# Mixture-of-experts FFN behind an adaptive layer norm: six of eight token blocks sorted by expert

## The chip, the cores and the metric

The kernel runs on one core of one Trainium2 chip. The metric is the device time of one execution in microseconds (us). Of the kernel before there are three timed runs: 565.57, 567.19 and 568.79 us, median 567.19. One more execution was profiled; it took 565.48 us, of which the traced span is 563.4 us.

Engines: PE multiplies matrices, DVE and POOL do elementwise work, ACT does activations and copies, SP only issues DMAs. POOL issues DMAs as well in the changed kernel. Each engine works through its own queue in order.

## The reference

There are 4096 tokens (128 batches of 32) of 128 features, all in fp32. Two layers, each a conditioning step and a feed-forward step with a residual:

```python
# layer 0: conditioning
U = (mu @ W_dec + b_dec).reshape(B, IN_DIM + 1, K)          # K = 30
param = jnp.einsum('bik,kj->bij', U, V)
out = jnp.einsum('bsd,bde->bse', x, param[:, :-1, :]) + param[:, -1, :][:, None, :]
# layer 0: mixture of 8 experts, the best two of each token
topk_scores, topk_idx = jax.lax.top_k(xf @ Wg.T + bg, K)    # K = 2
w = jax.nn.softmax(topk_scores, axis=-1)
h = jax.nn.gelu(jnp.einsum('td,ehd->teh', xf, W1) + b1[None], approximate=False)
o = jnp.einsum('teh,eoh->teo', h, W2) + b2[None]            # all experts, hidden 256
out = jnp.einsum('tko,tk->to', jnp.take_along_axis(o, topk_idx[:, :, None], axis=1), w)
# layer 1: conditioning by table look-ups, three layer norms and an MLP; then
h = jax.nn.silu(_tlin(x, w1_w, w1_s)) * _tlin(x, w2_w, w2_s)          # 128 -> 512
h = jax.nn.gelu(_tlin(h, h1_w, h1_s), approximate=False)              # 512 -> 512
h = jax.nn.gelu(_tlin(h, h2_w, h2_s), approximate=False)              # 512 -> 512
out = _tlin(h, w3_w, w3_s)                                            # 512 -> 128
```

A token needs only two experts of eight; computing all eight gives the same sum with six weights of zero.

## The kernel before

The tokens are split into NB = 8 blocks of TB = 512. Features lie on the partitions, tokens along the free dimension.

**Setup.** The conditioned token of layer 0 has rank 30, so `conditioned(i)` (L221) computes a 32-row vector z per token (`pz`, L225; `zT`, L233), splits it into a rounded half and a remainder [...], and stacks it four times over 128 partitions (`z4s[i]`, L245). `folded_all` (L210) folds V and W1 into `w4`. The gate scores `pg` (L308) come from `z4s`; `routing` (L252) is a chain of some 30 DVE operations over [128, 32 x 8] that finds the best two experts of every token and writes their weights into `hot4` (L300, L301).

**Experts.** `experts(i)` (L473) goes through all 8 experts for its 512 tokens. For each expert: one matmul `pbc` (L491) that spreads the token's weight for this expert over the partitions; and for both 128-row halves of the hidden layer a matmul `ph` (L495, fp32r), a Gelu on ACT (`hs`, L497), a product with `pbc` on DVE (`hw`, L499), and a matmul in full fp32 that accumulates into `po` (L500). The fp32 matmul appears as two records in the trace.

**Conditioning.** `conditioning(i)` (L511) makes the input of the second feed-forward step from `x1T`: transposes, three layer norms (`layernorm`, L394, with two small POOL operations L402 and L403; the norm of `h` also scales its four tiles on POOL, L405), table look-ups as one-hot matmuls (`ppw`, L542), an MLP (`pi`, L577 to L596) and the result `cT` (L608). `halves` (L617) splits it: a cast on ACT (L620) and a subtraction on POOL (L622).

**Feed-forward.** `feed_forward(i)` (L631) has four layers. `pf` gives four `ga` tiles through `gated` (L625: one ACT and two DVE operations each), then `pgb` and `pgc` give four tiles each with a Gelu on ACT (L666). All these matmuls are fp32r at L638, and each activation is split by `halves` for the layer after it. At the end `oT` (L677), a transpose `pot` (L680), a copy and a store.

**Order.** The generators yield between steps, and `beside` (L51) interleaves the streams given to it in proportion to their step counts. A scheduler that works with estimated durations then lays the instructions out on each engine, the earlier emitted first where several are ready; on the chip each queue is fixed. The main loop runs three streams at a time and waits for all of them:

```python
for i in range(NB):
    streams = [(feed_forward(i), 14)]
    if i + 1 < NB: streams.append((conditioning(i + 1), 13))
    if i + 2 < NB: streams.append((experts(i + 2), 18))
    beside(*streams)
```

Before it `experts(0)` runs beside the loading of the feed-forward weights (L360, a POOL sum at L369) and the small second-layer weights (L422), then `experts(1)` beside `conditioning(0)`.

Of the kernel before, what the change touches and what calls it, by code (L numbers as in the profile page):

```python
# [16 lines left out]
P = 128  # L17
# [13 lines left out]
VPW = 125  # L31
EPS = 1e-5
# [18 lines left out]
def beside(*streams):  # L51


    left = [[s, n, 0] for s, n in streams]
    while left:
        e = min(left, key=lambda e: (e[2] + 0.5) / e[1])
        e[2] += 1
        if next(e[0], e) is e:
            left.remove(e)
# [3 lines left out]
def adaln_ffn_kernel(ctx: ExitStack, tc: tile.TileContext, a, out: bass.AP):  # L63
# [32 lines left out]
    def rows(tag, n):  # L96

        t = const.tile([P, n], F32R, tag=tag, name=tag)
        nc.gpsimd.memset(t.bitcast(F32), 0.0)
        return t  # L100
# [12 lines left out]

    early = ctx.enter_context(ExitStack())
    setup = early.enter_context(tc.tile_pool(name="setup", bufs=1))
# [8 lines left out]
    bias_rows = load("bias_rows", [1, E * H + E], eng=nc.scalar, pool=setup)  # L124
    w1_t = load("moe_w1", [D, E * H], pool=setup)
    x_all = setup.tile([D, NB, TB], F32, tag="x_all", name="x_all")
    for i in range(NB):
        nc.sync.dma_start(x_all[:, i, :], a["x_t"][:, i * TB : (i + 1) * TB])
    tabs = load("tabs", [4 * E, NTAB], eng=nc.scalar, pool=setup)
    vecs = load("vecs", [P, NVEC], eng=nc.scalar)  # L130
    w2_t = load("moe_w2", [P, E, NH, D])
    int_w1 = load("int_w1", [P, 6, D], a["int_w1"].rearrange("(i p) j -> p i j", p=P))
    aw_bc = load("aw", [P, 6], a["aw"].partition_broadcast(P), eng=nc.scalar)
    st_a = load("st_a", [64, 4, D], eng=nc.scalar)
    st_b = load("st_b", [32, 2, D], eng=nc.scalar)
    wide_w2 = load("wide_w2", [D, 4, D])
    b2_rows = load("b2_rows", [1, 3 * D], eng=nc.scalar)
    tab_b = load("tab_b", [D, 3, 16], eng=nc.scalar)
# [17 lines left out]
    def stacked(dst, src, r, tmp):  # L156
# [3 lines left out]
        hi = tmp.tile([n, dst.shape[1]], F32R, tag="hi", name=f"hi_{dst.tensor.name}", bufs=2)  # L160
# [8 lines left out]
    twice = const.tile([2 * KZ, 2, 2 * KZ], F32R, tag="twice", name="twice")  # L169
# [31 lines left out]
    g4 = const.tile([P, E], F32R, tag="g4", name="g4")  # L201

    def folded(dst, w, bias, name):
        n = dst.shape[1]
        pv = ps_acc(name)
        nc.tensor.matmul(pv[:, :n], pre[:, V4 : V4 + P], w, start=True, stop=False)
        nc.tensor.matmul(pv[:, :n], bias_at, bias, start=False, stop=True)
        stacked(dst, pv[:, :n], 64, setup)

    def folded_all():  # L210
        folded(g4, pre[:, WG : WG + E], bias_rows[:, E * H :], "pgv")
# [38 lines left out]
    hot4 = const.tile([P, NCH, 4, E], F32, tag="hot4", name="hot4")  # L250

    def routing(pg):  # L252

        def t8(name, dt=F32):
# [590 lines left out]
```

## Time and profile before

| | us |
|---|---|
| median of three runs | 567.19 |
| the profiled execution | 565.48 |
| its span, first to last instruction | 563.4 |
| setup and routing, up to the first `pwT` | 0 to 63.4 |
| experts 0 and 1, conditioning 0, up to the first `cT` | 63.4 to 143.1 |
| feed-forward 0 to 5, each beside experts and conditioning | 143.1 to 476.9 |
| feed-forward 6 beside conditioning 7 | 476.9 to 518.9 |
| feed-forward 7 alone, and the end | 518.9 to 563.4 |

Busy share of the span: PE 88%, DVE 51%, ACT 42%, POOL 37%. In the profile, busy time of PE counts each matmul with its passage through the array, and neighbours overlap; how long PE needs per matmul is read from the distance between the ends of successive ones. "PEclk" is the granted clock of PE, 1.00 being full speed. A wait is put down to the instruction that released it.

### The profile page before, as it was taken

The page shows a single profiled execution, that of the slowest core. Times are in us where ns is not written, and L with a number is a line of the kernel's source. Part 1 is how long each engine was busy: PE and PEld are TensorE (multiplying, and loading weights), DVE is VectorE, ACT ScalarE, POOL GpSimd, SP SyncE. Part 2 cuts the span into 40 slices and gives each one's busy share as a digit, 9 for nine tenths or more (in the row PEclk, how much of TensorE's full clock was granted, in tenths as well). Part 3 has the DMA queues.
Part 4 walks back from the last instruction along what each step waited for, and adds up shares of the span by engine and source line. Part 5 has one row for each costly group of instructions (what it writes and reads, how often), then busy time and mean ns, then how long its engine had stood idle before and what let it go on. Part 6 is the DMA issues. An engine that isn't in the chain of part 4 may idle for free. (4 is left out here: it accounts for less than half of the span.)

```text
span 563.4 us, 5941 instructions
## 1 busy us (share of the span) xinstructions
PE 497.5 (88%) x1997; PEld 310.3 (55%) x1997; DVE 289.0 (51%) x689; ACT 235.4 (42%) x412; POOL 209.4 (37%) x226
## 2 busy tenths in 40 slices
PE   5998587979899979997999799979997999689694
PEld 5963243534566546654665466546654665365373
DVE  2875786744763565356535653565356535623400
ACT  0141553322455344534453455345534552353343
POOL 3000065030373237323722372237223722384353
PEclk9985599989899999999999999999999999899588
DMA  8800330100100020002000200020001000100100
GB/s 209 298 11 3 113 110 1 39 19 5 53 19 2 2 74 19 0 3 74 19 1 3 74 19 0 5 74 18 1 1 57 0 1 1 56 0 1 37 0 24
DMA packets 14634, 20.46 MB, mean 36 GB/s; under 512 B 1632, under 2 KB 7358, under 8 KB 14342
## 3 DMA queue, kind: packets, MB, share of 16 engines
q1 hardware_dynamic: 13762, 19.56, 10.9%
q10 hardware_dynamic: 836, 0.47, 0.4%
q8 instruction: 18, 0.29, 0.2%
q14 instruction: 18, 0.14, 0.1%
HBM read 13.72 MB, written 6.29 MB: 36 GB/s over the span
## 5 line engine op out<-in xcount | busy, mean ns | idle before, releaser
L500 PE MATMUL po<-hw,moe_w_sb 128*128 128x512 f32 x256 | 135.8, 627 | 8.7 <-DVE hw L499 8.7
L499 DVE TENSOR_TENSOR hw<-hs,pbc 128x512 f32<-128x512 f32 x128 | 85.9, 681 | 67.7 <-PE pbc L491 35.0
L497 ACT ACTIVATE hs<-ph 128x512 f32<-128x512 f32 x128 | 74.6, 596 | 55.2 <-PE ph L495 31.8
L622 POOL TENSOR_TENSOR gc_lo<-gc,gc_hi 128x512 fp32r<-128x512 f32 x32 | 40.7, 1273 | 95.8 <-ACT gc_hi L620 95.2
L500 PEld LDWEIGHTS po<-hw,moe_w_sb 128*128 128x128 f32 x256 | 44.2, 193 | 48.4 <-DVE hw L499 36.5
L622 POOL TENSOR_TENSOR ga_lo<-ga,ga_hi 128x512 fp32r<-128x512 f32 x32 | 41.0, 1280 | 68.9 <-ACT ga_hi L620 68.9
L495 PE MATMUL ph<-z,w 128*128 128x512 f32 x128 | 53.2, 442 | 2.5 <-ACT hs L497 2.5
L622 POOL TENSOR_TENSOR gb_lo<-gb,gb_hi 128x512 fp32r<-128x512 f32 x32 | 40.5, 1287 | 18.8 <-ACT gb_hi L620 16.6
L638 PE MATMUL pgc<-gb_lo,f_h_hi 128*128 128x512 f32 x128 | 44.8, 454 | 1.4 <-POOL gb_lo L622 1.3
L638 PE MATMUL pgb<-ga_hi,f_h_hi 128*128 128x512 f32 x128 | 42.7, 447 | 1.3 <-DVE sl L628 1.3
L666 ACT ACTIVATE gb<-pgb,vecs_sb 128x512 f32<-128x512 f32 x32 | 22.0, 689 | 50.1 <-PE pgb L638 50.1
L638 PE MATMUL pgc<-gb_hi,f_h_hi 128*128 128x512 f32 x128 | 41.0, 437 | 0.1
L666 ACT ACTIVATE gc<-pgc,vecs_sb 128x512 f32<-128x512 f32 x32 | 22.0, 689 | 45.4 <-PE pgc L638 45.4
L627 ACT ACTIVATE sl<-pf,half_w1s 128x512 f32<-128x512 f32 x32 | 22.0, 688 | 43.8 <-PE pf L638 41.1
L638 PE MATMUL pf<-cT_hi,f_w_hi 128*128 128x512 f32 x64 | 32.8, 534 | 8.3 <-DVE sl L628 5.9
L638 PE MATMUL pgb<-ga_lo,f_h_hi 128*128 128x512 f32 x128 | 39.4, 422 | 0.1
L491 PE MATMUL pbc<-w_rows,pick 128*128 128x512 f32 x64 | 36.9, 577 | 0.0
L628 DVE SCALAR_TENSOR_TENSOR sl<-sl,pf 128x512 f32<-128x512 f32 x32 | 21.7, 679 | 20.5 <-ACT sl L627 20.3
L638 PEld LDWEIGHTS pgb<-ga_hi,f_h_hi 128*128 128x128 f32 x128 | 24.8, 196 | 12.9 <-issue 4.1
L638 PEld LDWEIGHTS pgc<-gb_lo,f_h_hi 128*128 128x128 f32 x128 | 24.1, 188 | 13.9 <-issue 6.0
L495 PEld LDWEIGHTS ph<-z,w 128*128 128x128 f32 x128 | 24.9, 196 | 12.1 <-ACT hs L497 6.5
L638 PE MATMUL pf<-cT_lo,f_w_hi 128*128 128x512 f32 x64 | 27.8, 442 | 3.7 <-POOL cT_lo L622 3.6
(230 smaller groups left out, 810.2 us busy)
## 6 DMA issues: line engine op xcount, KB each, us to landing
moe_w_sb<-in_moe_w_dram SPq DMA_DIRECT2D x2, 1024.0 KB
x_all<-in_x_t_dram SPq DMA_DIRECT2D x8, 256.0 KB
xT<-in_x_t_dram SPq DMA_DIRECT2D x8, 256.0 KB
f_h_raw<-in_f_h_dram SPq DMA_DIRECT2D x8, 256.0 KB
kept_x<-x1T SPq DMA_DIRECT2D x8, 256.0 KB
kept_c<-cT SPq DMA_DIRECT2D x8, 256.0 KB
out_dram<-o SPq DMA_DIRECT2D x8, 256.0 KB
pid<-in_pid_dram SPq DMA_DIRECT2D x8, 250.0 KB
```

Source lines behind the costliest of these rows:

```text
L491: nc.tensor.matmul(pbc, pick[:, e, :], wr, start=True, stop=True)
L495: nc.tensor.matmul(ph, w4[:, c : c + P], z4, start=True, stop=True)
L497: nc.scalar.activation(hs, ph, AF.Gelu)
L499: nc.vector.tensor_tensor(hw, hs, pbc, ALU.mult)
L500: nc.tensor.matmul(po, w2_t[:, e, h, :], hw, start=False, stop=(e == E - 1 and h == NH - 1))
L622: nc.gpsimd.tensor_tensor(lo, src, hi, ALU.subtract)
L627: nc.scalar.activation(tmp, p1, AF.Tanh, scale=half_w1s[:, f : f + 1])
L628: nc.vector.scalar_tensor_tensor(tmp, tmp, 1.0, p1, ALU.add, ALU.mult)
L638: nc.tensor.matmul(dst, w[:, c, f * P : (f + 1) * P], src[c][h], start=(k == 0), stop=(k == len(terms) - 1),)
L666: nc.scalar.activation(t, ph, AF.Gelu, scale=col(s + f))
```

## The change

- Blocks 0 and 1 keep the dense path over all experts. For blocks 2 to 7 the z vectors are transposed to one row per token (`z_tok`), and `sorting` computes on the chip, for each of a token's two experts, its place in that expert's list (a matmul with a triangle of ones, and a prefix sum over the 24 groups of 128 tokens).
- 48 indirect DMAs, issued by POOL, scatter the rows of z (256 B each, 128 rows per DMA) into `z_rows` in DRAM, which was zeroed by eight DMAs from SP. Each expert has a fixed CAP of 1024 rows.
- `sorted_expert` runs 16 tiles of 512 rows, two per expert: two loads of the rows, four transposes, two `ph` matmuls, two Gelus, eight pairs' worth of 128-wide fp32 matmuls into `py`, an add of the bias, and a store to `y_rows` in DRAM.
- `combined(i)` reads the block's rows back: eight indirect DMAs per block on POOL, each followed by a DVE multiply-add onto x; then four transposes give `x1T`. In these blocks the first layer norm reads the sum directly, so the transposes at L522 are not made.
- The gate scores come from `zT` in full fp32 instead of the stacked z. The norm of `h` is scaled on DVE instead of POOL.
- The streams are put in order by start and length in a virtual time (`in_order`), no longer in groups that wait for each other. Conditioning i ends half a unit ahead of feed-forward i.
- If an expert gets more than 1024 rows, a conditional block at the end computes blocks 2 to 7 again by the dense path. With these inputs the six blocks give the experts 766, 662, 729, 818, 757, 715, 929 and 768 rows, so it isn't entered.

The core of the diff:

```diff
--- before.py
+++ after.py
+ND = 2
+NS = NB - ND
+TS = 512
+CAP = 1024
+ALL = NS * TB
+NT_S = E * CAP // TS
...
-def beside(*streams):
-    left = [[s, n, 0] for s, n in streams]
-    while left:
-        e = min(left, key=lambda e: (e[2] + 0.5) / e[1])
-        e[2] += 1
-        if next(e[0], e) is e:
-            left.remove(e)
+def in_order(*streams):
+    times = [(t + d * k / n, j) for j, (t, d, n, _) in enumerate(streams) for k in range(n)]
+    for _, j in sorted(times):
+        next(streams[j][3], None)
+    for *_, s in streams:
+        for _ in s:
+            raise ValueError("more steps than were given")
...
+    x_t = []
+    for i in range(NB):
+        x_t.append(setup.tile([D, TB], F32, tag=f"x_t{i}", name=f"x_t{i}"))
+        nc.sync.dma_start(x_t[i], a["x_t"][:, i * TB : (i + 1) * TB])
     w1_t = load("moe_w1", [D, E * H], pool=setup)
-    x_all = setup.tile([D, NB, TB], F32, tag="x_all", name="x_all")
-    for i in range(NB):
-        nc.sync.dma_start(x_all[:, i, :], a["x_t"][:, i * TB : (i + 1) * TB])
+    z_rows = kept.tile([E * ALL, 2 * KZ], F32, tag="z_rows", name="z_rows")
+    zeros = setup.tile([P, TB], F32, tag="zeros", name="zeros")
+    nc.gpsimd.memset(zeros, 0.0)
+    for e in range(E):
+        nc.sync.dma_start(
+            z_rows[e * ALL : e * ALL + CAP].rearrange("(p c) k -> p (c k)", p=P), zeros
+        )
...
+        pv = ps_acc("pgv")
+        nc.tensor.matmul(
+            pv[:KZ, :E], pre[:, V4 : V4 + KZ], pre[:, WG : WG + E], start=True, stop=False
+        )
+        nc.tensor.matmul(
+            pv[:KZ, :E], bias_at[:, :KZ], bias_rows[:, E * H :], start=False, stop=True
+        )
...
+        for c in range(NC):
+            nc.tensor.matmul(
+                pg[:, (i * NC + c) * E : (i * NC + c + 1) * E],
+                zT[:, c * P : (c + 1) * P],
+                gv,
+                start=True,
+                stop=True,
+            )
...
+            pt = ps_mm(f"pzt_{i}")
+            for c in range(NC):
+                nc.tensor.transpose(
+                    pt[:, c * KZ : (c + 1) * KZ], zT[:, c * P : (c + 1) * P], ident[:KZ, :KZ]
+                )
+            z = z_tok[i - ND]
+            both = pt[:, : NC * KZ].rearrange("p (c k) -> p c k", k=KZ)
+            nc.scalar.copy(z[:, :, 0, :], both)
+            nc.vector.tensor_tensor(z[:, :, 1, :], both, z[:, :, 0, :], ALU.subtract)
+            nc.sync.dma_start(
+                z_kept[i - ND].rearrange("(c p) k -> p c k", p=P),
+                z.rearrange("p c r k -> p c (r k)").bitcast(F32),
+            )
...
+    def sorting(hots):
+        n, c0 = NS * NC, ND * NC
+        h = [t[:, c0:] for t in hots]
+        both = setup.tile([P, n, E], F32R, tag="both", name="both")
+        nc.vector.tensor_tensor(both, h[0], h[1], ALU.add)
+        flat = both.rearrange("p c e -> p (c e)")
+        pr = ps_mm("p_rank")
+        nc.tensor.matmul(pr[:, : n * E], before, flat, start=True, stop=True)
+        pn = ps_ff("p_count")
+        nc.tensor.matmul(pn[:, : n * E], ones_r, flat, start=True, stop=True)
+        src, dst = sums
+        nc.vector.tensor_copy(src[:, PRE:], pn[:, : n * E].rearrange("p (c e) -> p c e", e=E))
+        d = 1
+        while d < n:
+            nc.vector.tensor_tensor(
+                dst[:, PRE:], src[:, PRE:], src[:, PRE - d : PRE - d + n], ALU.add
+            )
+            src, dst = dst, src
+            d *= 2
+        row = setup.tile([P, n, E], F32, tag="row", name="row")
+        nc.vector.tensor_tensor(
+            row,
+            pr[:, : n * E].rearrange("p (c e) -> p c e", e=E),
+            src[:, PRE - 1 : PRE - 1 + n],
+            ALU.add,
+        )
+        row_z = setup.tile([P, n, E], F32, tag="row_z", name="row_z")
+        nc.vector.scalar_tensor_tensor(
+            row_z, iota_e.to_broadcast([P, n, E]), float(ALL), row, ALU.mult, ALU.add
+        )
+        nc.vector.scalar_tensor_tensor(
+            row, row, float(CAP - 1), first_row.to_broadcast([P, n, E]), ALU.min, ALU.add
+        )
+        for name, src_row, dsts in (("z", row_z, row_best_z), ("y", row, row_best)):
+            for j in range(2):
+                at = setup.tile([P, n, E], F32, tag="row_at", name=f"row_at{name}{j}")
+                nc.vector.tensor_tensor(at, src_row, h[j], ALU.mult)
+                row_f = setup.tile([P, n], F32, tag=f"row_f{j}", name=f"row_f{name}{j}")
+                nc.vector.tensor_reduce(row_f, at, AX.X, ALU.add)
+                nc.vector.tensor_copy(dsts[j], row_f)
+        nc.vector.tensor_reduce(most, src[:1, PRE + n - 1], AX.X, ALU.max)
...
+    folding = folded_all()
+    next(folding)
+    in_order(
+        (1.5, 6.0, 4, folding),
+        *((float(i), 1.5, 2, conditioned(i)) for i in range(NB)),
+    )
+    hots = routing()
+    sorting(hots)
+    token_weights(hots)
+    y_rows = kept.tile([E * CAP, D], F32, tag="y_rows", name="y_rows")
+    for c in range(NS * NC):
+        for j in range(2):
+            scatter = nc.gpsimd.indirect_dma_start(
+                z_rows,
+                bass.IndirectOffsetOnAxis(ap=row_best_z[j][:, c : c + 1], axis=0),
+                z_tok[c // NC][:, c % NC].rearrange("p r k -> p (r k)").bitcast(F32),
+                None,
+            )
...
-    def layernorm(dst, src, n, name, eng=None):
+    def layernorm(dst, src, n, name):
...
-            (eng or nc.vector).tensor_scalar(
+            nc.vector.tensor_scalar(
...
+        hi = dense.tile([P, NC, E], F32R, tag="w_hi", name=f"w_hi{i}")
+        w = w_hot[:, i * NC : (i + 1) * NC]
+        nc.vector.tensor_copy(hi, w)
+        hot4 = dense.tile([P, NC, 4, E], F32, tag="hot4", name=f"hot4_{i}")
+        for h in (0, 2):
+            nc.vector.tensor_copy(hot4[:, :, h, :], hi)
+            nc.vector.tensor_tensor(hot4[:, :, h + 1, :], w, hi, ALU.subtract)
...
+    def sorted_expert(t, b2_all):
+        e, n = t * TS // CAP, TS // P
+        here = slice(t * TS, (t + 1) * TS)
+        zr = exp.tile([P, n, 2, 2 * KZ], F32, tag="zr", name=f"zr{t}", bufs=2)
+        first = e * ALL + t * TS % CAP
+        z_here = z_rows[first : first + TS].rearrange("(p c) k -> p c k", p=P)
+        for r in range(2):
+            nc.sync.dma_start(zr[:, :, r, :], z_here)
+        pt = ps_bc(f"pzr{t}")
+        for c in range(n):
+            nc.tensor.transpose(
+                pt[:, c * P : (c + 1) * P], zr[:, c].rearrange("p r k -> p (r k)"), ident
+            )
+        z4 = exp.tile([P, TS], F32R, tag="z4", name=f"zs{t}", bufs=2)
+        nc.vector.tensor_copy(z4, pt)
+        yield
+        hs = []
+        for h in range(NH):
+            ph = ps_mm(f"phs{t}_{h}")
+            c = (e * NH + h) * P
+            nc.tensor.matmul(ph, w4[:, c : c + P], z4, start=True, stop=True)
+            hs.append(exp.tile([P, TS], F32, tag="hs", name=f"hss{t}_{h}", bufs=3))
+            nc.scalar.activation(hs[h], ph, AF.Gelu)
+        yield
+        py = ps_acc(f"py{t}")
+        for c in range(n):
+            for h in range(NH):
+                nc.tensor.matmul(
+                    py[:, c * D : (c + 1) * D],
+                    hs[h][:, c * P : (c + 1) * P],
+                    w2_t[:, e, h * D : (h + 1) * D],
+                    start=(h == 0),
+                    stop=(h == NH - 1),
+                )
+        y = exp.tile([P, n, D], F32, tag="y", name=f"y{t}", bufs=2)
+        nc.vector.tensor_tensor(
+            y,
+            py.rearrange("p (c d) -> p c d", d=D),
+            b2_all[:, e : e + 1, :].to_broadcast([P, n, D]),
+            ALU.add,
+        )
+        nc.sync.dma_start(y_rows[here].rearrange("(p c) d -> p c d", p=P), y)
+        yield
+    def sorted_experts():
+        b2_all = exp.tile([P, E, D], F32, tag="b2_all", name="b2_all", bufs=1)
+        nc.sync.dma_start(b2_all, a["moe_b2"].partition_broadcast(P))
+        live = []
+        for t in range(NT_S + 2):
+            if t < NT_S:
+                live.append(sorted_expert(t, b2_all))
+            for s in live[::-1]:
+                next(s)
+            if t >= 2:
+                live.pop(0)
+            yield
+    def combined(i):
+        toks = slice(i * TB, (i + 1) * TB)
+        x1 = work.tile([P, NC, D], F32, tag="x1", name=f"x1_{i}", bufs=2)
+        nc.sync.dma_start(x1, a["x"][toks].rearrange("(c p) d -> p c d", p=P))
+        for c in range(NC):
+            ch, sc = i * NC + c, (i - ND) * NC + c
+            for j in range(2):
+                yg = work.tile([P, D], F32, tag="yg", name=f"yg_{i}_{c}_{j}", bufs=8)
+                nc.gpsimd.indirect_dma_start(
+                    yg,
+                    None,
+                    y_rows,
+                    bass.IndirectOffsetOnAxis(ap=row_best[j][:, sc : sc + 1], axis=0),
+                )
+                nc.vector.scalar_tensor_tensor(
+                    x1[:, c, :], yg, w_best[j][:, ch : ch + 1], x1[:, c, :], ALU.mult, ALU.add
+                )
+        st[i] = {"x1": x1}
+        yield
+        pt = transpose_tiles(x1, f"px1_{i}")
+        x1T = work.tile([D, TB], F32, tag="x1T", name=f"x1T_{i}", bufs=3)
+        nc.scalar.copy(x1T, pt)
+        nc.sync.dma_start(kept_x[i], x1T)
+        st[i]["x1T"] = x1T
+        yield
...
-        layernorm(h1, h1, NC, f"h_{i}", eng=nc.gpsimd)
+        layernorm(h1, h1, NC, f"h_{i}")
...
-    beside((experts(0), 18), (feed_forward_weights(), 11), (second_layer_weights(), 8))
-    count_unequal()
-    beside((conditioning(0), 13), (experts(1), 18))
-    for i in range(NB):
-        streams = [(feed_forward(i), 14)]
-        if i + 1 < NB:
-            streams.append((conditioning(i + 1), 13))
-        if i + 2 < NB:
-            streams.append((experts(i + 2), 18))
-        beside(*streams)
+    tiles = dense_tiles()
+    in_order(
+        (0.0, 1.0, 18, experts(0, z4s[0], w4, w2_t, *tiles)),
+        (0.0, 1.0, 11, feed_forward_weights()),
+        (0.0, 1.0, 8, second_layer_weights()),
+        (1.0, 0.1, 1, count_unequal()),
+        (1.0, 1.0, 18, experts(1, z4s[1], w4, w2_t, *tiles)),
+        (1.0, 0.9, 13, conditioning(0, False)),
+    )
+    dense_stack.close()
+    sorted_stack = ctx.enter_context(ExitStack())
+    exp = sorted_stack.enter_context(
+        tc.tile_pool(name="exp", bufs=1, side="right", reuse_waits="tile")
+    )
+    in_order(
+        (2.0, 1.2, NT_S + 2, sorted_experts()),
+        (2.0, 0.9, 13, conditioning(1, False)),
+        (2.0, 1.1, 14, feed_forward(0)),
+        (3.1, 1.2, 14, feed_forward(1)),
+        (3.3, 0.7, 15, conditioning(2, True)),
+        *((i + 0.9, 0.9, 15, conditioning(i, True)) for i in range(3, NB)),
+        *((i + 2.3, 1.0, 14, feed_forward(i)) for i in range(2, NB)),
+    )
+    sorted_stack.close()
     inner.close()
-    n_unequal = nc.values_load(any_unequal[0:1, 0:1], min_val=0, max_val=1)
-    with tc.If(n_unequal > 0):
+    is_special = nc.values_load(special[0:1, 0:1], min_val=0, max_val=1)
+    with tc.If(is_special > 0):
...
```

## The prediction

> **What bounds the kernel now.** I read the engine totals and the 40 slices first, then the costliest groups, the DVE instructions `oT` as stage marks, the busy table of the stages between them, and last PE's instructions in order of time.
>
> ```profile
> PE 497.5 (88%) x1997; PEld 310.3 (55%) x1997; DVE 289.0 (51%) x689; ACT 235.4 (42%) x412; POOL 209.4 (37%) x226
> PEclk9985599989899999999999999999999999899588
> ```
>
> PE leads, at full clock all through the middle. The `oT` marks stand at 194.4, 250.9, 307.4, 363.9, 420.4 and 476.9: a constant period of 56.5 us per block.
>
> ```profile
> 420.40:476.90 56.50, 52.81 (x199) 32.98 (x197) 28.87 (x70) 26.21 (x46) 23.24 (x23) 1.00 0.04 15
> 476.90:518.90 42.00, 35.65 (x137) 23.25 (x136) 17.77 (x51) 18.27 (x29) 22.57 (x23) 0.96 0.05 19
> 518.90:563.40 44.50, 31.08 (x100) 20.06 (x100) 9.39 (x15) 16.85 (x27) 17.31 (x14) 0.77 0.06 20
> 63.40:143.10 79.70, 67.50 (x207) 33.95 (x208) 51.48 (x115) 30.39 (x56) 24.81 (x27) 0.93 0.13 40
> 48.00:63.40 15.40, 8.20 (x10) 1.98 (x10) 10.79 (x33) 2.72 (x6) 0.00 (x0) 0.50 0.27 87
> ```
>
> Columns: stretch, length, busy PE, weight load, DVE, ACT, POOL, then the granted clock. Row 1 is a full block. Row 2 is the same without experts: 42.0, and no engine is full. Row 3 is a feed-forward alone. Row 5 is routing, where PE runs at half clock.
>
> What PE really needs follows from the ends of neighbours:
>
> ```profile
> 323.92 0.40 PE L495 MATMUL ph<-z,w 128*128 128x512 f32 x1
> 324.15 1.88 PE L500 MATMUL po<-hw,moe_w_sb 128*128 128x512 f32 x4
> 325.47 0.79 PE L491 MATMUL pbc<-w_rows,pick 128*128 128x512 f32 x1
> ...
> 515.76 1.16 PE L596 MATMUL pi<-half_int_w,aT 128*128 128x128 f32 x8
> ```
>
> Ends at 324.32, 326.03 and 326.26: an fp32 record of 512 columns takes 1.71/4 = 0.43, an fp32r one 0.23. The eight 128-wide fp32 records of L596 end 1.0 after their predecessor, 0.125 each. A transpose takes 0.09 (four `pot` start at 308.49, the next `ph` at 308.84). Per block PE needs: experts 32 x 0.43 + 24 x 0.23 + 0.6 = 19.9; feed-forward 88 x 0.23 + 0.35 = 20.6; conditioning about 8 (16 transposes 1.4, `ppw` 1.0, five fp32r 1.2, eight fp32 records of `pi` 3.4, `p2` 1.0). Sum 48.5 of 56.5, or 86%: PE sets the period.
>
> **The experts' work.** Six dense blocks go: 6 x 19.9 = 119 us of PE. A sorted tile costs 4 x 0.09 + 2 x 0.23 + 16 x 0.125 = 2.8, and 16 tiles 45. PE saves 74 us at full clock. DVE loses 96 `hw` of 0.68 (65 us) and gains 32 operations of [128, 512] from PSUM at 0.69 (22; the row of `x1T`, L505), 48 multiply-adds of 128 columns at 0.29 (14; the row of `st_act`, L447) and the 32 tiles of the `h` norm at 0.40 (13): 16 less. ACT loses 64 Gelus of 0.60 (38 us). POOL loses the 25.2 of L405 and gets 96 indirect DMAs. No tile stays behind a scarce PSUM bank: the sorted tiles use the banks that dense experts used.
>
> **The price of an indirect DMA on POOL**, c, is in no row. A plain DMA holds SP's queue some 0.3 us (`kept_c`, 0.33), the lower end; POOL's own [128, 4] power, L403, takes 1.01. The Trainium skill (DMA: Bandwidth & Descriptors, "Anatomy of one DMA — SWDGE (gpsimd) path") puts about 2.0 us fixed on a POOL-issued DMA, most of it latency after issue. Against the change speaks the skill's SBUF — State Buffer ("SBUF: two separate sides"): POOL writes these descriptors through a port that some DVE instructions lock, and one such DMA grew from about 0.62 to 3.1 us. The nearest thing in this trace is mild: `ga_lo` on POOL takes 1.27 to 1.29 beside a busy DVE. By the row, c = 1.1 and all 96 cost POOL 106 us; by the page's worst, 3.1 and 298. I take 1.1, near L403, and keep 0.3 to 3.1 for the range.
>
> **Setup.** SP gets eight zeroing DMAs of 256 KB, 2.1 MB; at the 248 GB/s of the first 21 us that is 8.5 us behind x and w1, ahead of `moe_w2`, which is first needed after routing: hidden. Without that cover it would cost 8.5. In fp32, `pg` takes 64 short records for 32 and the transposes 24 x 0.09; some 5 us more before routing, less the stacking of six blocks (six `p4` and casts): +4. Routing saves the `hot4` tail before the sort but adds it per block later; its gaps in the old trace (DVE waiting at 50.5 and 56.8 for `hi_w`, 2.2 each) close, since folding now ends before `pg`. Sorting adds some 25 DVE operations at about 0.35 plus two PE round trips at half clock, 10. Sum: 4 + 10 - 4.4 - 4 = about +5, so the first `pwT` moves from 63.4 to 68; between 0 and +12.
>
> **Scatters and the dense stage.** All 48 wait for the routing chain and come ahead of the other POOL work of the stage by emission: from 64 to 64 + 48c = 117. Behind them queue the sums of L369, the small norms of the second-layer weights and `rs_x` of conditioning 0. Their POOL time before was 24.8, less 3.2 of `h`: 22. So POOL's work lasts to about 139 at least, and `rs_x` can't come before 117; in the 42.0 stage `cT` came 35 after `rs_x` (486.4 to 521.4). 117 + 35 = 152 for `cT` 0 instead of 143. Experts 0 and 1 themselves need no POOL; their 40 us of PE work and the routing weights go on beside the scatters.
>
> **Sorted stage.** Experts in 16 tiles, feed-forward 0 and conditioning 1: 45 + 20.6 + 8 = 74 us of PE; at the old 86%, 86. Some 15 us of tiles can run in the hole that POOL leaves PE before 152 (they need the scatters only). 152 + 71 = 223.
>
> **Units.** Feed-forward 1 to 6 each beside a conditioning. The nearest row is the 42.0 stage, in which feed-forward 6 itself ran from its first `pf` (479.7) to `oT` (518.9), 39.2; the rest is the wait for the next `cT`, which in the new order is ready half a unit early. Taking `h` off POOL saves the 1.3 that PE waited for `gb_lo` at 504 to 506 behind its 3.15; eight gathers put 8c = 9 us on POOL, which is idle half of this stage, so about 2 show as delay of a `lo`. 39.8 x 6 = 239: 462. **Tail:** feed-forward 7 alone and the end, 44.5 less the 2.5 at its start: 42. Span 504. The clock of the units should lie nearer row 2's 0.96 than row 3's 0.77; the 42.0 already holds it.
>
> Sum: the span changes by 504 - 563.4 = -59. The profiled execution took 2.1 over its span and the median of runs 1.7 over that: 504 + 4 = 508 us.
>
> **Rivals.**
> 1. *PE keeps its 86%.* If feed-forward steps of successive blocks overlap, a unit is 28.6/0.86 = 33 and the sorted tiles fill holes: 508 - 6 x 6.5 = 469. For: decoupled streams. Against: in 42.0 PE was at 28.6, 68%, waiting on chains ACT, DVE, ACT, POOL between layers.
> 2. *Chains bind.* Gathers sit in front of the `lo` subtractions at full cost and no tile fills a hole: 15 + 6 x 5 more, 508 + 45 = 553. For: POOL would hold 20 + 9 of 40 in each unit, and each layer waits for its last `lo`.
> 3. *POOL is the bound: slower.* At c = 3.1 scatters end at 213, `cT` 0 comes at about 248, the sorted stage 335, units of POOL 20 + 25 = 45: 335 + 270 + 42 + 4 = 651. It decides from about c = 1.7: from there 48(c - 1.1) of delay and 6 x 8(c - 1.1) exposed, 96 x 0.6 = 58, eat the gain.
> 4. *The sort changes nothing on PE*: excluded, the list of 8192 rows is fixed.
>
> **How the numbers follow.** Chances: my sum 0.48, rival 1 0.18, rival 2 0.19, rival 3 0.15. Rival 2 is faster still in most of its width. My own case lies within 485 to 530 (setup 0 to 12, c between 0.8 and 1.4). Range 462 to 570: below it some 0.07 of rival 1, above it 0.13 of rival 3. Within 0.5% of 567, about what these runs can tell from no change, 0.02; slower 0.15; faster 0.83.
>
> **What would show it.** Right: an `oT` spacing of 38 to 42 from block 2 on, PE total down from 497 to about 420 to 440, `pwT` at 64 to 75, scatters on POOL back to back for about 53 us, and `cT` 0 near 150. Wrong: scatters that last beyond 150; PE waiting for `z4` or `zr`; `lo` on POOL waiting behind gathers; a gap at the end of the last `y` store before the first gather lands; a clock near 0.75 in the units.

## The result and the profile after

The changed kernel takes 610.73 us, the median of four runs (608.78 to 614.83), against 567.16 for the kernel before. The ratio is 1.078 (95% interval 1.071 to 1.085): 44 us slower, where 508 us were forecast. The profiled execution took 608.78 us, its span is 607.0. In what follows ratios leave disturbed executions out, so where the runs of a kernel spread (e8, e10, e11, e13, e15) a ratio can differ from the quotient of the medians, and the traces of e10 and e15 are of such executions (592.18 and 569.74 us).

The page of the changed kernel, the engine totals and three rows of its 40 slices (15.2 us a digit):

```profile
PE 445.2 (73%) x2035; PEld 308.5 (51%) x2035; DVE 295.3 (49%) x729; ACT 202.1 (33%) x341; POOL 282.0 (46%) x294
...
PE   6999387001389799999577468738988879878894
...
POOL 4000057778500242140888665773454645635453
PEclk9997589655589899999668788976998999989998
```

PE works 52 us less than before (445.2 for 497.5), just above the 420 to 440 of the forecast. So the saving is there and the time is not: PE has a hole of 0, 0, 1 in its eighth to tenth slice, where POOL has 7, 7, 8, and a second dip from the 20th on, 5, 7, 7, 4, 6, where POOL has 8, 8, 8, 6, 6. Both are stretches of indirect DMAs. POOL itself is busy 46% of the span.

The table by stage (length, busy PE, weight load, DVE, ACT, POOL, granted clock, DMA share, GB/s), in order of time; from row 4 on the bounds are `oT` of blocks 0, 1, 2, 3 and 4:

```profile
104.60:145.00 40.40, 0.40 (x2) 0.00 (x0) 0.67 (x1) 0.00 (x0) 31.53 (x34) 0.56 0.10 35
145.00:204.00 59.00, 41.23 (x130) 22.31 (x130) 37.16 (x91) 13.98 (x26) 17.96 (x20) 0.78 0.13 39
204.00:276.00 72.00, 69.06 (x433) 58.37 (x433) 39.40 (x87) 33.76 (x57) 21.63 (x20) 0.98 0.43 120
276.00:356.40 80.40, 52.85 (x208) 36.58 (x207) 40.13 (x105) 22.30 (x37) 54.45 (x53) 0.79 0.21 61
356.40:409.60 53.20, 35.06 (x138) 23.22 (x137) 27.90 (x71) 18.33 (x30) 35.99 (x35) 0.91 0.16 45
409.60:452.00 42.40, 36.57 (x137) 24.48 (x136) 27.61 (x65) 18.34 (x30) 20.40 (x19) 0.87 0.09 32
452.00:491.70 39.70, 33.87 (x138) 23.41 (x139) 21.82 (x59) 18.43 (x30) 20.10 (x19) 0.96 0.08 28
```

Row 1 is the hole: PE does 0.40 us of work in 40.4. Row 3, the sorted stage, takes 72.0 us at full PE, row 7 is a unit as forecast, 39.7. Rows 4 and 5 are units of 80.4 and 53.2 instead, and POOL carries 54.45 and 35.99 in them.

Who waits in the hole, from the view of waits (us in total, times, longest):

```profile
PE pst L578 <- DVE st_hat L528: 48.1, 3, 40.9
DVE st_hat L528 <- POOL rs_st L526: 43.1, 3, 40.2
```

The transposes `pst` of the second-layer weights wait for `st_hat` on DVE, and this for `rs_st`, two tiny POOL operations. On POOL they stand behind all 48 scatters, which run from 80.0 to 142.2 us. PE's queue is in order, so the experts of block 1, which need nothing of it, stand behind `pst`.

And the second dip, POOL's queue in order of time in feed-forward 1 (start, length), then one PE instruction of the same stretch:

```profile
294.34 1.30 POOL L857 TENSOR_TENSOR ga_lo<-ga,ga_hi 128x512 fp32r<-128x512 f32 x1
295.80 0.96 POOL L723 DMA_INDIRECT yg<-y_rows,row  x1 [0.16 <-issue]
297.06 0.94 POOL L723 DMA_INDIRECT yg<-y_rows,row  x1 [0.30 <-PE px L536]
298.30 0.94 POOL L723 DMA_INDIRECT yg<-y_rows,row  x1 [0.30 <-issue]
299.55 0.94 POOL L723 DMA_INDIRECT yg<-y_rows,row  x1 [0.30 <-issue]
300.50 1.28 POOL L857 TENSOR_TENSOR ga_lo<-ga,ga_hi 128x512 fp32r<-128x512 f32 x1
```

```profile
301.84 0.80 PE L873 MATMUL pgb<-ga_lo,f_h_hi 128*128 128x512 f32 x1 [4.06 <-POOL ga_lo L857]
```

The `ga_lo` at 300.50 stands behind four gathers, and PE waits 4.06 us for it. All 48 gathers lie in feed-forward 1 and 2, 32 and 16 of them, between 288 and 408 us among the `lo` subtractions: the scheduler put them in early, those of the later blocks two units and more ahead of their conditioning (block 7's begin at 395, its conditioning's first norm at 519).

### The profile page after: what moved, and what is told of

Its sections match the earlier page's. It is cut to its first block, busy times and chain, and to the rows that moved or that the text cites. A ratio compares the mean times of both kernels' runs of the same rounds, so it can differ in the third digit from the quotient of the medians.

```text
span 607.0 us, 6207 instructions
## 1 busy us (share of the span) xinstructions
PE 445.2 (73%) x2035; PEld 308.5 (51%) x2035; DVE 295.3 (49%) x729; ACT 202.1 (33%) x341; POOL 282.0 (46%) x294
## 5 line engine op out<-in xcount | busy, mean ns | idle before, releaser
L436 POOL DMA_INDIRECT z_rows<-z_tok,row_z x48 | 47.9, 998 | 87.4 <-DVE row_z L403 73.1
L857 POOL TENSOR_TENSOR ga_lo<-ga,ga_hi 128x512 fp32r<-128x512 f32 x32 | 40.9, 1280 | 77.3 <-ACT ga_hi L855 74.4
L723 POOL DMA_INDIRECT yg<-y_rows,row x48 | 48.2, 1003 | 22.0 <-DVE x L729 10.2
L873 PE MATMUL pgb<-ga_lo,f_h_hi 128*128 128x512 f32 x128 | 42.6, 439 | 6.2 <-POOL ga_lo L857 6.2
L873 PE MATMUL pgb<-ga_hi,f_h_hi 128*128 128x512 f32 x128 | 43.6, 448 | 2.4 <-DVE sl L863 1.4
L873 PE MATMUL pgc<-gb_lo,f_h_hi 128*128 128x512 f32 x128 | 37.5, 407 | 7.0 <-POOL gb_lo L857 6.9
L873 PE MATMUL pf<-cT_hi,f_w_hi 128*128 128x512 f32 x64 | 34.7, 545 | 10.8 <-DVE sl L863 7.8
L641 PE MATMUL po<-hw,moe_w_sb 128*128 128x512 f32 x64 | 34.6, 648 | 6.7 <-DVE hw L640 6.7
L873 PE MATMUL pgc<-gb_hi,f_h_hi 128*128 128x512 f32 x128 | 39.1, 412 | 0.3
L873 PEld LDWEIGHTS pgb<-ga_lo,f_h_hi 128*128 128x128 f32 x128 | 26.2, 207 | 15.3 <-POOL ga_lo L857 9.8
L683 PEld LDWEIGHTS py<-moe_w_sb,hss 128*128 128x128 f32 x256 | 31.1, 191 | 2.2 <-ACT hss L678 0.7
L683 PE MATMUL py<-moe_w_sb,hss 128*128 128x128 f32 x256 | 32.0, 276 | 0.1
L873 PEld LDWEIGHTS pgc<-gb_lo,f_h_hi 128*128 128x128 f32 x128 | 24.4, 191 | 14.8 <-POOL gb_lo L857 9.8
L873 PEld LDWEIGHTS pgb<-ga_hi,f_h_hi 128*128 128x128 f32 x128 | 24.2, 200 | 13.8 <-ACT ga_hi L855 4.6
L638 ACT ACTIVATE hs<-ph 128x512 f32<-128x512 f32 x32 | 18.8, 597 | 34.3 <-PE ph L636 16.2
```

Of the source, the lines that this page charges most:

```text
L436: scatter = nc.gpsimd.indirect_dma_start(z_rows, bass.IndirectOffsetOnAxis(ap=row_best_z[j][:, c : c + 1], axis=0), z_tok[c // NC][:, c % ...
L638: nc.scalar.activation(hs, ph, AF.Gelu)
L641: nc.tensor.matmul(po, w2_t[:, e, h * D : (h + 1) * D], hw, start=False, stop=(e == E - 1 and h == NH - 1),)
L683: nc.tensor.matmul(py[:, c * D : (c + 1) * D], hs[h][:, c * P : (c + 1) * P], w2_t[:, e, h * D : (h + 1) * D], start=(h == 0), stop=(h == ...
L723: nc.gpsimd.indirect_dma_start(yg, None, y_rows, bass.IndirectOffsetOnAxis(ap=row_best[j][:, sc : sc + 1], axis=0),)
L857: nc.gpsimd.tensor_tensor(lo, src, hi, ALU.subtract)
```

## The experiments

Two theories. **A**: the loss is POOL's queue order: work that PE waits for stands behind indirect DMAs. **B**: it is the sorted path itself, its trips through DRAM and PE's slower clock. Later runs divide A further: is it the order that can be mended, or POOL's time, which is paid wherever a DMA stands? All times are from runs beside the kernel before. Two marks divide each trace: `oT` of block 0, and the way from there to `oT` of block 6 (six units).

| kernel | `oT` 0 | `oT` 0 to 6 | median us | ratio (interval) |
|---|---|---|---|---|
| changed kernel | 276.0 | 294.3 | 610.73 | 1.078 (1.071 to 1.085) |
| e1 plain scatters | 225.6 | 294.5 | 560.12 | 0.989 (0.986 to 0.992) |
| e2 plain gathers | 285.6 | 246.3 | 566.52 | 0.999 (0.995 to 1.003) |
| e3 both plain | 229.3 | 249.8 | 515.47 | 0.911 (0.906 to 0.916) |
| e4 scatters spread | 254.8 | 295.5 | 587.12 | 1.031 (1.026 to 1.037) |
| e5 scatters spread, gathers tied late | 251.9 | 324.8 | 618.47 | 1.093 (1.087 to 1.098) |
| e6 gathers paced | 273.6 | 298.4 | 614.32 | 1.082 (1.079 to 1.086) |
| e7 = e4 with e6 | 252.1 | 299.4 | 592.59 | 1.041 (1.035 to 1.047) |
| e8 = e7, second-layer weights first | 253.3 | 298.3 | 596.85 | 1.055 (1.048 to 1.063) |
| e9 = e4, gathers early, adds tied | 254.5 | 295.2 | 588.11 | 1.035 (1.027 to 1.043) |
| e10 = e9, POOL freed of other work | 256.4 | 296.7 | 583.43 | 1.013 (1.008 to 1.019) |
| e11 = e9, one `lo` in four on DVE | 254.5 | 278.6 | 571.52 | 1.005 (1.001 to 1.009) |
| e12 = e11, conditioning 0 later | 269.5 | 274.8 | 585.79 | 1.032 (1.026 to 1.039) |
| e13 all of it, two `lo` in four | 253.5 | 269.5 | 564.02 | 0.993 (0.989 to 0.996) |
| e14 = e13, scatters in short runs | 269.6 | 269.4 | 582.22 | 1.027 (1.023 to 1.031) |
| e15 = e14, count last | 263.1 | 266.4 | 565.41 | 0.997 (0.995 to 0.999) |

### e1, e2, e3: the same bytes without POOL

Each indirect DMA becomes a plain one from SP, to or from fixed rows, so the placement by expert is left out and all other work stays.

```diff
-            scatter = nc.gpsimd.indirect_dma_start(z_rows, rows_z, z_tok, None)
+            nc.sync.dma_start(z_rows[r0 : r0 + P], z_tok)              # e1, e3
-                nc.gpsimd.indirect_dma_start(yg, None, y_rows, rows)
+                nc.sync.dma_start(yg, y_rows[k * P : (k + 1) * P])     # e2, e3
```

> The 48 indirect scatters on POOL become plain DMAs from SP to fixed rows (so the rows are not sorted: the placement by expert is left out). Theory A, POOL's fixed queue: the small norms of the second-layer weights no longer stand behind 62 us of scatters, PE's wait of 41 us for st_hat goes, and so does most of the slow 20 us after it; cT 0 comes near 153 instead of 204 and the time falls from 611 to 555-570. Theory B, the sorted path itself (DRAM round trips, cold clock): the scatters are only cover for other waits, 595 or more.

> The 48 indirect gathers on POOL become plain loads of fixed rows from SP (the selection of the token's own rows is left out). Theory A: the 40 gathers that stand among the lo subtractions of feed-forward 1 and 2 go; the stages of 80 and 53 us fall to about 45 and 42, the later units stay near 39; 611 becomes 560-572. Theory B: those stages are slow because the conditioning waits for y_rows to land in DRAM; they stay above 65 and 48 and the time above 590.

> Both edits at once; POOL issues no DMA. Theory A: the two gains add, 508-525, near the sum that the prediction made. Theory B: above 580. If the sum of gains is much less than that of the two single runs, one wait covered the other.

Measured: 50.6 us less than the changed kernel, 44.2 less, and 95.3 less together. The parts add, each in its own stretch: e1 gains before `oT` 0 (50.4) and nothing in the units, e2 gains 48.0 in the units, and loses 9.6 ahead of them, where nothing was edited (`pwT` alone comes 5.9 later). B falls: the sorted path with its DRAM trips stays in e3. That e3 comes within 8 us of the forecast doesn't confirm it, since the forecast had the indirect DMAs in it. The 95 us go with the indirect DMAs on POOL. These runs don't tell order from time.

### e4 and e5: mending the order

e4 makes the scatters a stream of the dense stage, two to a step, each held behind the last small POOL operation written so far. e5 does this, writes the gathers two to a step, and ties each behind the last `lo` subtraction written.

```diff
+    def scatters():
+        for c in range(NS * NC):
+            for j in range(2):
+                with tc.issue_after(last_pool[0]): scatter(c, j)
+            yield
+        (0.05, 1.7, 24, scatters()),
-                nc.gpsimd.indirect_dma_start(yg, ...)
+                with tc.issue_after(last_lo[0]): nc.gpsimd.indirect_dma_start(yg, ...)   # e5
```

> The full function; of the two moves of the run with both orders, the scatters' alone (two a step, each queued behind the last small POOL operation; the gathers as in the changed kernel). If the dense stage's stall is POOL's queue order, cT of block 0 comes near 179 us again in place of 204, the wait for block 1's and 2's gathers stays, and the time is 610.7 - 25 = 586 us (580 to 592). If the scatters only carry their delay elsewhere: over 600.

> Full function, all 96 indirect DMAs stay on POOL. Scatters are emitted two at a time through the dense stage and each is queued behind the small POOL operations emitted before it; gathers are emitted two at a time and each is queued behind the last lo subtraction emitted before it. Theory A: only the order was wrong, not the price; the time falls to 520-545, first cT near 165, feed-forward 1 and 2 at 45-50. Theory B, or POOL's sum of work as the bound: 580 or more.

e4 is as expected: `cT` of block 0 at 182.4 for 204.2, and 23.6 us less in the median. Waits of PE for `st_hat` of 20.5 us remain, up to 11.7 at once. e5 missed by 73 us: its units 2 to 5 are 52 to 58 us long. The waits from `oT` 0 to `oT` 5 of e5:

```profile
DVE x L740 <- DMA yg<-y_rows,row: 58.9, 25, 9.3
```

The gather now came late, its multiply-add stood next to it on DVE, and DVE's queue, through which every `ga` goes, waited up to 9.3 us for it. The wait had moved to another engine.

### e6, e7, e8: gathers paced through the unit

Gathers are a stream, one to a step, the multiply-add written three steps later. e8 also writes the second-layer weights first and starts the scatters later. In these three the last of block 2's eight additions is written after its sum is read, so that sum lacks it; the instructions are all there.

```diff
+    def gathering(i):
+        for k in range(8 + 3):
+            if k < 8:
+                with tc.issue_after(last_lo[0]): gather(k)
+            if k >= 3: multiply_add(k - 3)
+            yield
+        *((i + 0.4, 0.6, 11, gathering(i)) for i in range(4, NB)),
-        (0.05, 1.7, 24, scatters()),  (0.0, 1.0, 8, second_layer_weights()),    # e8
+        (0.4, 1.3, 24, scatters()),  (0.0, 0.45, 8, second_layer_weights()),
```

> The full function; scatters as in the changed kernel. The eight gathers of a block are a stream of their own: one to a step, not before the last lo subtraction written, and its multiply-add three steps later, so that neither POOL nor DVE waits for it. If the loss of ff1 and ff2 is the order of POOL's queue (and the run with both orders lost on the multiply-adds standing too close to their gathers), units are 40 to 42 us and the time is that of plain loads plus a few: 566.5 to 580 us. If gathers cost their POOL time wherever they stand (8 x 1.27 = 10 us a unit), units are 48 to 52 us and the time stays at 605 to 640.

> The full function; scatters moved as in the first run of this list and gathers as in the second. By the order theory both gains add: 610.7 - 25 - 40 = 546 us (538 to 556), below the kernel before. If gathers cost their POOL time wherever they stand: 580 or more.

> As the run before it, with the second-layer weights in the first 0.45 of the dense stage and the scatters from 0.4 on, so that the three small normalisations meet no scatter. By the order theory cT of block 0 comes at 160 to 175 us rather than 179, and the time is 530 to 546 us. If the end of the scatters (they start later, 48 x 1.27 = 61 us) is what starts the sorted stage, it is no better than the run before: 546 to 556.

All three missed. The way from `oT` 0 to 6 is 298 to 299, not shorter than with the gathers in a heap: feed-forward 1 fell from 80.4 to 61.7, and units 3 to 5 rose to 47 to 48. The scheduler drew the multiply-adds forward again, beside their gathers: over the same stretch of e6 the waits show

```profile
DVE x L737 <- DMA yg<-y_rows,row: 42.6, 22, 6.0
```

So order alone was not yet tried cleanly. e8 left the dense stage as it was (`cT` 0 at 181.6): PE now waited 8.4 us for `h` behind other scatters.

### e9 and e10: gathers early, and a free POOL

e9 ties a gather 16 to 9 `lo`'s back (8 to 1 for blocks 2 and 3), some 20 us ahead of use, and its multiply-add behind the last gated product on DVE. e10 also writes the second-layer weights first, makes their three small normalisations one and moves the `unequal` additions to DVE.

```diff
+                with tc.issue_after(los[-max(1, (16 if i > 3 else 8) - 2 * c - j)]): gather(c, j)
+                with tc.issue_after(last_ga[0]): multiply_add(c, j)
+            if i == 2: layernorm(hat, p2_all, 3, "st")              # e10
-                nc.gpsimd.tensor_tensor(unequal, unequal, raw, ALU.add)
+                nc.vector.tensor_tensor(unequal, unequal, raw, ALU.add)
```

> The full function, scatters two a step as before. A gather of block 3 is tied behind the lo subtraction 8 to 1 places back, of blocks 4 to 7 behind that 16 to 9 places back, some 20 us ahead of its use; its multiply-add is tied behind the last gated product on DVE, so the schedule can't set it beside its gather. If what e6 lost was DVE standing at the multiply-adds (38.3 us from 300 to 560) and not POOL's 8 x 1.27 us a unit, units 3 to 6 are 39.5 to 42 us and the time is 545 us (535 to 558), below the kernel before. If POOL's own time is what a unit pays, units are 46 us or more and the time is 580 or more.

> As the run before it, and POOL freed in the dense stage: the three small normalisations of the second-layer weights are one, ahead of the scatters, and the 11 additions that count unequal weights go to DVE (14 us). By the order theory PE's waits for normalised rows behind scatters (24 us from 95 to 160 in the run with the second layer first) mostly go: cT of block 0 near 160 us rather than 180, and the time is 525 us (515 to 540). If DVE, with 7 us more, sets the dense stage instead: cT near 175 and 540 or more.

Now DVE's waits for `yg` are 5.8 us in all from 254 to 512, and the time is still that of e4: 588.11 for 587.12; both runs missed. Three units of e9, block 3 to 5:

```profile
376.90:423.70 46.80, 36.80 (x139) 24.62 (x139) 26.75 (x66) 19.03 (x31) 27.95 (x28) 0.90 0.12 40
423.70:468.40 44.70, 36.08 (x137) 24.24 (x135) 26.56 (x65) 17.67 (x29) 28.32 (x28) 0.89 0.12 37
468.40:512.20 43.80, 36.78 (x140) 24.85 (x139) 25.90 (x66) 18.92 (x31) 22.93 (x22) 0.88 0.07 23
```

In the first two POOL is busy 28 of 45 us, so it isn't full; yet these units, with eight gathers each, take 46.8 and 44.7 us, 7 and 5 more than one without (39.7, row 7 of the table by stage). The length less busy PE is the time in which PE stands: 10.0 and 8.6 us, for 5.8 in row 7. The rest is PE itself, busy 36 to 37 us for 33.87, at a granted clock of 0.90 and 0.89 for 0.96. The third unit holds two gathers only and still takes 43.8: PE stands 7.0 us there, and most of its excess is PE busy longer, at 0.88. Why the clock is lower, no run here isolates. Part of the standing is again a wait for `lo`, from 377 to 512:

```profile
PE pf L888 <- POOL gc_lo L870: 5.4, 4, 1.9
```

So gathers that stand singly still cost. The trace of e10 holds no gain: `cT` 0 is at 184.6, since PE, nearly free of `st_hat` (3.8 us), now waits 12.2 us at `pxh` of conditioning 0 for `rs_x`, which stands behind scatters in its turn. Where its smaller ratio comes from is not shown.

### e11 to e15: taking what PE waits for off POOL

e11: the last `lo` of each layer in blocks 1 to 5 goes to DVE. e12: conditioning 0 is written into the sorted stage. e13: two `lo`'s of four on DVE, e10's dense stage, and the first transposes of conditioning 0 tied on PE behind block 1's experts; its gathers are tied 12 POOL `lo`'s back in place of 16.

```diff
+        if on_dve: nc.vector.tensor_tensor(lo, src, hi, ALU.subtract)
+        # e11: f == NF - 1 and 1 <= i <= 5;  e13: f % 2 == 1 and 1 <= i <= 5
-        (1.0, 0.9, 13, conditioning(0, False)),                     # e12, dense stage
+        (2.0, 0.4, 13, conditioning(0, False)),                     # e12, sorted stage
+                with tc.issue_after(last_po[0]): transpose(px_0)    # e13
```

> As the run with gathers tied back (586.5 us span, units 3 to 5 of 46.8, 44.7 and 43.8 us), and in blocks 1 to 5 the last lo subtraction of each layer, the one PE needs first after a layer ends, goes to DVE (0.7 us) and so stands behind no gather. If a unit pays for its gathers through these lo's, units 3 to 5 fall to 40 to 42 us, ff1 and ff2 by some 8 together, and the time is 568 us (560 to 575). If DVE's queue holds them as long, or the price is not there (the granted clock, ACT): 580 to 592.

> As the run before it, and the conditioning of block 0 is written into the sorted stage instead of the dense one, so that PE's queue in the dense stage holds only the two blocks of experts and the second-layer weights while POOL scatters. If PE's waits for rs_x and rs_h behind scatters (12 + 8 us) are the dense stage's loss, both blocks of experts end near 158 us rather than 182, the sorted work covers the conditioning, oT of block 0 comes near 240 us rather than 254, and the time is 554 us (545 to 562). If the conditioning of block 0 is then late for ff0: oT of block 0 at 250 or later and no gain.

> The full function. Dense stage: one normalisation for the second-layer weights, ahead of 40 of the scatters; the unequal additions on DVE; the conditioning of block 0 in the sorted stage, and its first transposes tied on PE behind the last product of block 1's experts, so that nothing on PE waits for POOL while it scatters. Units: in blocks 1 to 5 two of four lo subtractions of each layer on DVE, gathers one to a lo, some 12 lo's ahead. If the losses are order, x1T of block 1 comes at 155 to 162 us (181 in the last run), oT of block 1 near 302 (324), units 3 to 5 at 40 to 42 us, and the time is 550 us (540 to 560), below the kernel before. If POOL's time is paid wherever it stands: x1T of block 1 at 175 or later, units at 43 to 44, and 570 or more.

e11 gained 16.6 us, in the units and in the time alike; the time is within the range expected, though units 3 and 4 (43.6 and 43.0) are not quite. They hold eight gathers each; PE waits for no `lo` in them any more and stands 7.3 and 6.6 us, but is still busy 36.4 at 0.88:

```profile
369.30:413.00 43.70, 36.44 (x137) 24.96 (x137) 25.23 (x70) 18.86 (x31) 25.05 (x25) 0.88 0.15 43
413.00:456.00 43.00, 36.42 (x137) 24.68 (x137) 25.70 (x69) 18.22 (x30) 24.93 (x24) 0.88 0.12 38
```

Fewer `lo`'s on POOL alone win nothing: unit 5 of e11, which holds no gather, takes 39.4, that of the changed kernel 39.1. With e13 units 3 to 5, which hold 8, 8 and 2 gathers, are those of plain loads (39.4, 41.1, 40.5; in e3 40.2, 41.4, 39.1):

```profile
362.80:402.20 39.40, 34.02 (x137) 23.75 (x137) 26.35 (x68) 17.84 (x30) 21.04 (x21) 0.91 0.15 48
402.20:443.30 41.10, 33.94 (x137) 23.54 (x137) 26.32 (x71) 18.56 (x31) 21.04 (x21) 0.92 0.12 40
443.30:483.90 40.60, 33.86 (x137) 23.57 (x137) 26.34 (x72) 18.64 (x31) 14.84 (x15) 0.92 0.07 23
```

So in units 3 to 5 the price can be avoided with the gathers still on POOL, and from e9 to e11 it fell as PE's waits for `lo` went. The step from e11 to e13 is less plain: PE stands 5.4 and 7.2 us in units 3 and 4, and is busy 34 for 36.4 at a clock of 0.91 and 0.92. Most of that gain comes with the clock, whose cause stays open. e12 missed: the scheduler drew `pxh` of conditioning 0 back among block 1's experts, and PE waited 16.4 us at it for `rs_x` behind scatters. e13's tie ended that, and x1T of block 1 came at 162.4 as expected (180.8 in e12); but `oT` 0 stayed at 253.5, as conditioning 0 now lies in the sorted stage, and the time was 564.02 us, 4 over the expected range. It is 0.7% faster than the kernel before; of the other full versions only e15 is faster too, by 0.3%.

e13 has two stops of DVE that no engine explains, during 38 scatters in a row; the second outlasts them by 1.7 us:

```profile
135.98 1.28 DVE L653 TENSOR_TENSOR hw<-hs,pbc 128x512 f32<-128x512 f32 x2 [7.18 <-remote]
151.43 1.28 DVE L653 TENSOR_TENSOR hw<-hs,pbc 128x512 f32<-128x512 f32 x2 [14.16 <-remote]
```

Both inputs of the second had been there since 140.74. e14 breaks the scatters into runs of seven at most, with the `unequal` additions on POOL between them; e15 also moves the count of unequal weights behind block 1's experts.

```diff
-        (0.0, 1.0, 24, scatters()),  (0.0, 1.0, 11, feed_forward_weights()),
+        (0.0, 1.6, 24, scatters()),  (0.0, 1.6, 11, feed_forward_weights()),
+        with tc.issue_after(last_x1T[0]): nc.vector.tensor_reduce(n, unequal, AX.X, ALU.add)   # e15
```

> As the run before it, but the 11 additions that count unequal weights are on POOL again (14 us) and spread over the dense stage, so that no more than six scatters follow each other. If the two stops of DVE (7 and 14 us at 129 and 137 us, named remote) belong to the unbroken run of scatters, they are gone, x1T of block 1 comes at 150 to 158 us although POOL has 14 us more, and the time is 556 us (550 to 562). If they come whenever DVE and scatters overlap, or POOL's total is the limit: x1T of block 1 at 162 or later and 564 to 575.

> As the run before it, and the count of unequal weights is written after block 1's experts, on DVE behind its x1T and on PE behind its last product, so that neither waits 19 us for POOL's last addition with experts behind it. If that wait was the whole loss of the last run, x1T of block 1 comes at 155 to 160 us (176), the sorted stage starts with it, and the time is 564 us (558 to 568); below 558 if DVE's stops, 21 us in the run before, are gone and were on the path. If POOL's total (76 us from 80 on) holds the sorted stage: x1T of block 1 near 157 and oT of block 0 still at 258 or later, 570 or more.

The stops are gone in both, yet e14 lost 18 us to a new wait of the old kind:

```profile
PE p_unequal L504 <- DVE over L506: 19.4, 1, 19.4
DVE n_unequal L502 <- POOL unequal L493: 20.8, 1, 20.8
```

The last addition stood behind the last scatters, and PE stood before the count. e15 took it away and got back 16.8 us, to 565.41: within its range, and no better than e13. Breaking the runs won nothing; whether POOL's 14 us of additions took back what the stops had cost (the last scatter starts at 162.95 in e14, at 148.77 in e13), these runs don't show apart.

## Why the prediction was wrong

The forecast span was 504; 607.0 came. Its own steps:

- **PE's work, the steady unit, the tail.** Nearly right: PE 445.2 in total (420 to 440), units 4 to 6 39.7, 39.1 and 39.5 (39.8), the tail 36.8 (42). But these units hold no gather, and the 39.8 had 2 us for eight.
- **"Some 15 us of tiles can run in the hole that POOL leaves PE before 152 (they need the scatters only)."** Wrong, and hidden by luck: the stage from `cT` 0 to `oT` 0 took 72.0 (71). No tile ran ahead of `cT` 0: the first `pzr` comes at 212.3, 8.7 us after block 1's dense `x1T` (203.64), and by the same 8.7 in e1, which has no scatter to wait for. (In e13, where `x1T` comes at 162.4 and `cT` 0 at 196.0, 80 of the 256 `py` records do run ahead.) In return PE was busy 96% of the stage, not 86, and three of the 16 tiles (48 of the `py` records) ran after it. What holds the tiles back was not tried.
- **The price c.** Right in kind: 1.27 us from one to the next (1.1 taken), made of 0.96 busy and 0.30 before the next. The skill's 3.1 us, from SBUF — State Buffer ("SBUF: two separate sides"), was not met: the means are 1.00 us, the longest 2.13. Of the two prices weighed, the row was the better guide.
- **"Setup ... about +5".** Mis-sized: `pwT` at 73.4, not 68, and the first scatter at 80.0, not 64, as the place of a row is known only after the sort. The gate scores `g` reach DVE at 62.07 (47.78 before). PE works almost without a gap to 62 us; the folding products, which partly followed `pg` before, stand ahead of its last part. No run tried this part alone.
- **"Experts 0 and 1 themselves need no POOL; their 40 us of PE work and the routing weights go on beside the scatters."** Here it broke. The sentence holds of the experts and fails of the queue: the step named the small norms of the second-layer weights as standing behind the scatters on POOL, and did not ask who waits for them. PE did, in order, 40.9 us at once. With the later start `cT` 0 came at 204.2, not 152: 52 us. e1 and e4 show the cause: without scatters on POOL it comes at 153.8, spread out at 182.4. So the forecast's 152 was already the time without any scatter.
- **"Eight gathers put 8c = 9 us on POOL, which is idle half of this stage, so about 2 show as delay of a `lo`."** Wrong twice. The scheduler didn't keep eight to a unit but put all 48 into two, which took 80.4 and 53.2 for 39.8; the six units cost 294.3, not 239: 55 us, of which e2 gives 48.0 to the gathers. And at eight to a unit, 5 to 7 us show, not 2 (e9: 46.8 and 44.7, 39.7 without): 4.2 and 2.8 of PE standing, the rest PE busy longer at a lower clock. An engine idle half the time can still stand in the way at the moment that counts: a `lo` is needed at once by a PE that has nothing else.

52 + 1 + 55 - 5 = 103, which is 607 - 504. Of the rivals, the second had the mechanism of the gathers ("in front of the `lo` subtractions at full cost") and priced it at 30 us. The third had the sign: POOL as the reason for a slower kernel. But it made it depend on a price above 1.7, and at 1.27 the order of the queue did it, with POOL at 46%. "`lo` on POOL waiting behind gathers" was among the signs listed, and is what rows 4 and 5 of the table show; so was a clock near 0.75 in the units (row 4: 0.79).

What stays open: e13 is 47.5 us longer than e3 (spans 561.5 and 514.0). Of this 24.2 lie before `oT` 0: in the full versions it comes at 252 at the earliest, 229 in e3. POOL's 62 us of scatters begin at about 80, and the sorted stage can't be finished without them; how much of the rest is still order was not separated. Another 19.7 lie in the units, all of it in feed-forward 1 and 2, which take 55.4 and 53.9 in e13 (48.0 and 41.2 in e3), with 16 and 14 gathers in them; this wasn't tried apart.

## What to carry to other kernels

Before work is added to an in-order queue, write down for each added instruction what will stand behind it, who waits for that, and what stands behind the one that waits; a busy share of 37 or 46% answers none of this. A plain transfer in place of the suspected one costs one run and gives about the most that any reordering can win (here 95 us, of which e13 got back 47), before any reordering is written. When a mended order gives nothing back, look at which engine waits now: e5, e6, e10, e12 and e14 each moved a wait to another place. In the units, what worked was to take the operation that PE needs at once off the queue. And before a longer stretch is put down to waits, look whether its engine is standing, or busy at a lower clock.

## What the hardware showed

An indirect DMA of 128 rows cost POOL 0.96 us and 0.30 more before the next could start, 1.27 in a row; most scatters and gathers are at this, also beside a busy DVE. The longest stand in e13, beside an unbroken row of DVE operations that read two tiles, most of them `unequal` and `f_h_raw`: four of the five from 103.66 to 112.83 took 2.27, 2.03, 2.69 and 1.49. The longest, and DVE in the same time:

```profile
109.83 2.69 POOL L442 DMA_INDIRECT z_rows<-z_tok,row_z  x1 [0.30 <-issue]
109.81 0.67 DVE L493 TENSOR_TENSOR unequal<-unequal,f_h_raw 128x512 f32<-128x512 f32 x1
110.41 0.67 DVE L492 TENSOR_TENSOR f_h_raw<-f_h_raw,f_h_hi 128x512 f32<-128x512 f32 x1
111.01 0.67 DVE L492 TENSOR_TENSOR f_w_raw<-f_w_raw,f_w_hi 128x512 f32<-128x512 f32 x1
```

Scatters above 1.5 us occur only in e10 (one, 2.13) and e13, the two kernels with the `unequal` additions on DVE. That DVE is the cause was not tried by itself.

DVE stopped, with no releaser that the profile names, for 7.2 and 14.2 us in e13 (38 scatters in a row), for up to 14.0 in e2 and 14.8 in e6 (48 in a row), and for 6.9 and 6.3 in e10 (up to 26). ACT stopped so for 9.5 us in e8, whose runs are of twelve at most. But the changed kernel (48 in a row) and e12 (22) have no such stop, nor have the others, with runs of ten and less. The cause is not settled.
